# Two additions moved into TensorE's bank, a convolution of fifteen taps, and another order of the opening

## The chip, the core and the metric

The kernel runs on one core of a Trainium2 chip. The core has five engines with queues of their own: TensorE (PE in the profile; its weight loads are PEld), VectorE (DVE), ScalarE (ACT), GpSimd (POOL) and SyncE (SP), which here issues most transfers. Sixteen DMA engines move data between DRAM and the on-chip memory. TensorE writes its results into PSUM, in banks of 512 float32 elements per partition; the other engines read them there.

The metric is the device time of one execution in microseconds (us). The kernel before takes 5532.96 us, the median of three runs (5527.49 to 5539.79 us). The profiled execution took 5528.8 us, and its span from first to last instruction is 5527.0 us.

## The reference

Input x has 4 images of 64 x 64 positions with 96 channels. Layer 0 is a convolution with a selective scan, layer 1 a linear attention with a small network behind it. What matters here, shortened:

```python
# layer 0, on group-normalised x; bilinear(x, W) is sign(x) @ (s * sign(W - mean)).T + b
xz = bilinear(x, W_in, s_in, b_in)           # 96 -> 2 x 192 channels
xp, z = split(xz)
t = sign(xp + move0_b)                       # 192 channels of signs
t = conv3x3(t, sc * sign(conv_W))            # 192 -> 192, padded by one
t = t + conv_b + rp_b0
t = where(t >= 0, t, prelu_a * t)            # PReLU
t = t + rp_b1 + xp                           # residual within the branch
xconv = silu(t)
# four scan directions k over L = 4096 positions: rows, columns, and both reversed
dts, Bs, Cs = bilinear(...)                  # from the signs of xconv
h = exp(dt * A) * h + dt * u * B             # 192 channels x 16 states, per position
y_k = sum over states of h * C, plus D * u
y = sum of the four y_k, layer norm, times silu(z), bilinear back to 96 channels
x1 = x + y
# layer 1
x2 = x1 + attention(layer_norm(x1))          # linear attention: no softmax
out = x2 + ffn(layer_norm(x2))               # fp8-rounded weights and inputs
```

## The kernel before

The program goes through the images ("b", 0 to 3). A prologue for each image makes the scan's inputs (statistics, projection, convolution, sign tables); 1536 scan steps of 128 rows x 1024 positions follow one another without a break; an epilogue for each image does the rest. Prologues and epilogues of other images are generators whose next piece is put between two scan steps. Only the first image's prologue (called alone) and the last image's epilogue have no scan beside them. Every engine works through its instructions in the order in which the program lists them.

The scan step. A tally of each engine's work decides at build time whether the product after a scan goes to VectorE or to GpSimd. Operations called through c.vec and c.gps are counted in it, those called through nc.vector or nc.scalar are not:

```python
lead = c.vec.us - c.gps.us
c.vec.us, c.gps.us = max(0.0, min(lead, 8.0)), max(0.0, min(-lead, 8.0))
pool = c.vec.us + 1.2 > c.gps.us + 2.4
...
c.vec.tensor_tensor_scan(h, dA, w, first, ALU.mult, ALU.add)
if pool:
    self.late = (w, h, cr)                       # GpSimd does w = h * cr in the next step
else:
    c.vec.tensor_tensor(w, h, cr, ALU.mult)
```

On ScalarE the decay dA = exp(dl * anm) of the next step, into one of two PSUM tiles, goes ahead of each scan; GpSimd makes the injection w = dl * bc four steps ahead; TensorE sums the products over the states.

The pools that the change meets (name, buffers):

```python
p = SimpleNamespace(
    w=pool("wp", 9), y=pool("yp", 2), cy=pool("cyp", 2), h=pool("hp", 2), ...
    f=pool("fp", 8), ..., dA=pool("dAp", 2, space=PSUM), ps=pool("psp", 1, space=PSUM),
)
```

The weights, at the start: all loads are issued first, most on SyncE. Those of anm (the scan's A, 24 loads whose runs in DRAM are one element long) are issued on ScalarE's queue:

```python
for g in range(NG):
    src = a["al"][...].rearrange("d k (q j) -> j d (k q)", j=4)
    for j in range(4):
        nc.scalar.dma_start(anm[j::4, g, :], src[j])
```

The prologue's projection. The 192 channels lie as two halves of 96; the signs of each go into a padded image tp of 66 x 66:

```python
for h in range(2):
    for q in range(NQ8):                         # eight pieces of 512 positions
        px, pz = bank(f"ix{h}{q}", 0)[0:96], bank(f"iz{h}{q}", 1)[0:96]
        for ps, c0 in ((px, 96 * h), (pz, DN + 96 * h)):
            nc.tensor.matmul(ps, c.winT[:, c0 : c0 + 96], xsT[:, cols], start=True, stop=True)
        yield
        nc.scalar.activation(tpad[h][...], px..., AF.Sign, scale=..., bias=...)
        sz = f32(f"sz{h}{q}").bitcast(BF16)[0:96, 0:512]
        nc.scalar.activation(sz, pz, AF.Sign, ...)
        c.later.store(c.szd[b][h][:, cols], sz)
```

The convolution, in 16 parts of 96 output channels x 512 positions. A part has 18 matmuls of 96 input channels. The next part's taps are mixed with what is left of the part before:

```python
taps = [(j, t) for j in range(2) for t in range(9)]
...
            nc.tensor.matmul(ps, c.cw[:, j, t, 96 * h : 96 * h + 96], tpad[j][...],
                             start=(j == 0 and t == 0), stop=(j == 1 and t == 8))
...
if s == 0:      # the part before: pz holds sign(x) @ W, v = acs * conv + acb, r = relu(conv)
    c.vec.scalar_tensor_tensor(pz, pz, pv[:, ph, S_X : S_X + 1], v, ALU.mult, ALU.add)
    if alone:
        c.vec.scalar_tensor_tensor(pz, r, c.oma[:, one(ph)], pz, ALU.mult, ALU.add)
elif s == 1 and not alone:
    nc.tensor.matmul(pz, c.omad[:, ph], r, start=False, stop=True, skip_group_check=True)
... # then sign, exp, ln, exp on ScalarE and u = pz * e on VectorE
# after the taps of a part:
v = ...   # VectorE if alone, else ScalarE
r = ...   # ScalarE
pz = ...  # the projection's matmul once more
```

The sign tables. Direction by direction, the signs go to DRAM (sgd), come back as g, are turned by TensorE, and go to DRAM again (gTd), from where the scan loads gT twice, the second time shifted by 16 columns:

```python
nc.sync.dma_start(gw[:, x, 0:48], c.sgd[b][k].rearrange("(p f) -> p f", p=128))
gp = ...                                          # four matmuls with ident8
nc.scalar.activation(t.bitcast(F8), gp[0:48], AF.Copy, saturate=False)
nc.sync.dma_start(c.gTd[b][k], t)
# in the scan:
nc.sync.dma_start(w[0:48], src)
nc.sync.dma_start(w[64:112, :, 0:28], src[:, :, 4:32])
```

The epilogue's last stage, eight pieces of 512 positions for each image:

```python
mm(ps, [(self.ms[2], tt)])                        # the attention's output, plus bias
yield
x2 = f32("x2")[0:96]
c.vec.tensor_tensor(x2, ps, x1, ALU.add)
```

And the opening, in which weights and the first prologue take turns:

```python
made, first = c.weights(), prologue(c, 0, c.xts)
lanes = [made, first]
while (0, 1) not in c.ready:
    interleave(lanes)
    c.later.tick()
```

Of the kernel before, what the change touches and what calls it, by code (L numbers as in the profile page):

```python
# [11 lines left out]
F32 = mybir.dt.float32  # L12
BF16 = mybir.dt.bfloat16
# [40 lines left out]
def hybrid_kernel(ctx: ExitStack, tc: tile.TileContext, a: dict, out: bass.AP):  # L54
# [71 lines left out]
    cw = ctile("cw", [96, 2, 9, DN], F8)  # L126
# [6 lines left out]
    sbias, cbias = ctile("sbias", [96, 2]), ctile("cbias", [96, 2])  # L133
# [24 lines left out]
    def weights():  # L158
# [28 lines left out]
        def transposed(dst, srcs):  # L187

            count[0] += 1
            ps = p.ps.tile([128, 1024], BF16, name=f"tps{count[0]}", tag=f"y{count[0] % 2}")  # L190
            at = 0
            for src in srcs:
                n, f = src.shape
                nc.tensor.transpose(ps[:f, at : at + n], src, identb[:n, :n])
                at += n
            nc.vector.tensor_copy(dst, ps[:f, 0:at], saturate=False if dst.dtype == F8 else None)

# [4 lines left out]
        cwf, cwn = ([[temp(f"{nm}{h}{i}", [96, s.stop - s.start]) for i, s in enumerate(cuts)] for h in range(2)] for nm in ("cwf", "cwn"))  # L202
        for ts, src in ((cwf, a["cw_t"].rearrange("p h t d -> p h (t d)")), (cwn, a["cw_n"])):
            for rows, h, s in halves(src):
                for i, cut in enumerate(cuts):
                    nc.sync.dma_start(ts[h][i][rows], s[:, cut])
# [33 lines left out]
        nc.sync.dma_start(bff[DM : DM + 1, :], a["bff"])  # L240
        nc.scalar.dma_start(pvd, a["pv"][:, :, SD : SD + 3 * NK])
# [6 lines left out]
        for g in range(NG):  # L248
            src = a["al"][32 * (g % 4) : 32 * (g % 4) + 32, g // 4].rearrange("d k (q j) -> j d (k q)", j=4)
            for j in range(4):  # L250
                nc.scalar.dma_start(anm[j::4, g, :], src[j])
# [3 lines left out]
        nc.vector.tensor_tensor(sbias, pv[:, :, B_X], pv[:, :, MOVE0], ALU.add)  # L255
# [4 lines left out]
        transposed(winT, [wis[:, t, :] for t in range(3)])  # L260
        yield
        part = temp("part", [96, 2, 2])
        for h in range(2):
            for i, cut in enumerate(cuts):
                nc.scalar.activation(
                    cw[:, h].rearrange("p t d -> p (t d)")[:, cut], cwf[h][i], AF.Sign, saturate=False
                )
                nc.vector.tensor_reduce(part[:, h, i : i + 1], cwn[h][i], AX.X, ALU.add, apply_absolute_value=True)
# [67 lines left out]
        nc.scalar.activation(anm, anm, AF.Exp)  # L336
        nc.vector.tensor_scalar(anm, anm, -1.0, None, ALU.mult)
# [95 lines left out]
def run(c):  # L433

    made, first = c.weights(), prologue(c, 0, c.xts)
    lanes = [made, first]
    while (0, 1) not in c.ready:
        interleave(lanes)
        c.later.tick()
# [40 lines left out]
def prologue(c, b, xts=None):  # L480
# [11 lines left out]
    with tc.tile_pool(name=f"xg_{b}", bufs=1) as xgp:  # L492
# [3 lines left out]
        with tc.tile_pool(name=f"cv_{b}", bufs=1) as cvp:  # L496
            xsT = cvp.tile([DM, L], F8, name=f"xsT_{b}", tag="xsT")
            tflat = [cvp.tile([96, (IH + 2) * (IW + 2)], F8, name=f"tp{h}_{b}", tag=f"tp{h}") for h in range(2)]
# [58 lines left out]
            for h in range(2):  # L557
                for q in range(NQ8):
                    cols = slice(512 * q, 512 * q + 512)
                    px, pz = bank(f"ix{h}{q}", 0)[0:96], bank(f"iz{h}{q}", 1)[0:96]  # L560
                    for ps, c0 in ((px, 96 * h), (pz, DN + 96 * h)):
                        nc.tensor.matmul(ps, c.winT[:, c0 : c0 + 96], xsT[:, cols], start=True, stop=True)
                    yield
                    nc.scalar.activation(
                        tpad[h][:, 1 + 8 * q : 9 + 8 * q, 1 : 1 + IW], px.rearrange("p (h w) -> p h w", w=IW),
                        AF.Sign, scale=pv[:, h, S_X : S_X + 1], bias=c.sbias[:, h : h + 1], saturate=False,
                    )
                    sz = f32(f"sz{h}{q}").bitcast(BF16)[0:96, 0:512]
                    nc.scalar.activation(
                        sz, pz, AF.Sign, scale=pv[:, h, S_Z : S_Z + 1], bias=pv[:, h, B_Z : B_Z + 1]  # L570
                    )
                    c.later.store(c.szd[b][h][:, cols], sz)
# [4 lines left out]
            taps = [(j, t) for j in range(2) for t in range(9)]  # L577
            one = lambda h: slice(h, h + 1)
            prev = turned = None
            two = c.p.dA.tile([128, CH], F32, name=f"cv2_{b}", tag="dA") if alone else None  # L580
# [24 lines left out]
            for n, part in enumerate(parts + [None]):  # L605
                if part:
                    h, q = part
                    nm = f"{h}{q}"
                    at = 512 * (n % 2)
                    ps = (two[:, at : at + 512] if alone else bank("cv" + nm, 0))[0:96]  # L610
                for s in range(4 if alone else 5):
                    if part:
                        per = 5 if alone else 4
                        for j, t in taps[per * s : min(18, per * s + per)]:
                            dy, dx = divmod(t, 3)
                            nc.tensor.matmul(  # L616
                                ps, c.cw[:, j, t, 96 * h : 96 * h + 96],
                                tpad[j][:, 8 * q + dy : 8 * q + dy + 8, dx : dx + IW],
                                start=(j == 0 and t == 0), stop=(j == 1 and t == 8),
                            )  # L620
                    if s == 0 and turned:
                        by_columns(*turned)
                        turned = None
                    if prev:
                        ph, pq, pz, v, r, pn = prev
                        if s == 0:
                            c.vec.scalar_tensor_tensor(pz, pz, pv[:, ph, S_X : S_X + 1], v, ALU.mult, ALU.add)
                            if alone:
                                c.vec.scalar_tensor_tensor(pz, r, c.oma[:, one(ph)], pz, ALU.mult, ALU.add)
                        elif s == 1 and not alone:  # L630

                            nc.tensor.matmul(pz, c.omad[:, ph], r, start=False, stop=True, skip_group_check=True)
# [37 lines left out]
        with tc.tile_pool(name=f"rw_{b}", bufs=1) as rw:  # L670
# [5 lines left out]
            g2 = rw.tile([128, 2, 320], F8, name=f"g_{b}", tag="g")  # L676
            gw = g2.bitcast(F32)
            for o in (1, 0):
# [74 lines left out]
                if o:  # L753
                    nc.gpsimd.memset(gw[:, :, 48:80], 0.0)
                for x, k in enumerate((o, o + 2)):
                    nc.sync.dma_start(gw[:, x, 0:48], c.sgd[b][k].rearrange("(p f) -> p f", p=128))
                    yield
                    yield
                    gp = bank(f"gp{k}", k // 2).rearrange("p (s f) -> p s f", s=4)
                    for s in range(4):  # L760
                        nc.tensor.matmul(
                            gp[:, s, :], g2[:, x, 48 * s : 48 * s + 128], c.ident8, start=True, stop=True
                        )
                    yield
# [33 lines left out]
class Epilogue:  # L798
# [237 lines left out]
    def last(self, ln):  # L1036
# [22 lines left out]
        while nxt:  # L1059
# [10 lines left out]
            mm(ps, [(self.ms[2], tt)])  # L1070
            yield
            x2 = f32("x2")[0:96]
            c.vec.tensor_tensor(x2, ps, x1, ALU.add)
# [54 lines left out]
class Scans:  # L1128
# [6 lines left out]
    def __init__(self, c):  # L1135
# [10 lines left out]
        self.us, self.gs, self.at, self.loaded, self.sums = {}, {}, -1, set(), {}  # L1146
# [214 lines left out]
    def run(self, back):  # L1361
# [11 lines left out]
        interleave(lanes)  # L1373
        for q in range(NQ):
            self.load_bc(0, self.bt, 0, 0, 0, q)
            self.load_bc(1, self.ct, 0, 0, 0, q)
# [124 lines left out]
```

## Time and profile before

| what | value |
| --- | --- |
| time, median of three | 5532.96 us |
| VectorE busy | 5025.5 us |
| GpSimd busy | 4975.1 us |
| ScalarE busy | 3568.5 us |
| TensorE busy (matmuls) | 3478.7 us |
| first tap of the convolution | 84.1 us |
| first step matmul of the scan's inputs | 233.0 us |
| first scan | 269.6 us |
| last scan step's product ends | about 5410 us |

Busy times are those of the whole profiled execution. A row of the profile's groups names a line of the kernel, an engine, an operation, what it writes and reads ("out<-in"), shapes and count, then the busy time, the mean of one in ns, and the idle time of the engine just before, with what ended it. Line 404 is the tally's helper, so many operations share it and are told apart by their tiles. In a timeline a row has start and duration in us; "SPq" and "ACTq" are transfers being issued, not run.

### The profile page before, as it was taken

How to read it: one execution, taken by the hardware profiler on the slowest of the kernel's cores; microseconds unless marked ns; L12 is line 12 of the kernel's file. 1: busy time of each engine (PE TensorE's matmuls, PEld its weight loads, DVE VectorE, ACT ScalarE, POOL GpSimd, SP SyncE). 2: the span in 40 equal slices, each digit the busy share in tenths (PEclk: the TensorE clock that was granted, in tenths of full speed). 3: DMA queues.
4: the chain of work that ended last, by engine and by line, in shares of the span. 5: the costliest groups of instructions: out<-in, count | busy, mean ns of one | idle time of the engine just before them, and what ended most of it. 6: DMA issues, size and time to landing. Idle time of an engine off the chain costs nothing. (4 is left out here: it accounts for less than half of the span.)

```text
span 5527.0 us, 62184 instructions
## 1 busy us (share of the span) xinstructions
PE 3478.7 (63%) x20133; PEld 1371.3 (25%) x20133; DVE 5025.5 (91%) x3198; ACT 3568.5 (65%) x5568; POOL 4975.1 (90%) x2255
## 2 busy tenths in 40 slices
PE   6456765467645776657665677664677664445677
PEld 2222222122222232222222232221232221111223
DVE  3299999999999999999999999999999999999984
ACT  4467766677666667777666666776556775555554
POOL 2199999899999999999999999999999999999981
PEclk8666776678777776767876777765787565666777
DMA  4455765767666666676765666667666566666652
GB/s 80 120 191 187 211 204 189 237 220 211 200 192 207 197 199 207 195 237 212 223 191 184 206 205 195 198 208 229 201 214 194 179 194 199 213 202 190 204 157 60
DMA packets 613243, 1069.92 MB, mean 194 GB/s; under 512 B 225083, under 2 KB 343924, under 8 KB 611124
## 3 DMA queue, kind: packets, MB, share of 16 engines
q1 hardware_dynamic: 599428, 1065.88, 62.0%
q8 instruction: 158, 2.59, 0.2%
q10 hardware_dynamic: 13488, 0.07, 0.1%
q14 instruction: 169, 1.38, 0.1%
HBM read 833.20 MB, written 229.38 MB: 192 GB/s over the span
## 5 line engine op out<-in xcount | busy, mean ns | idle before, releaser
L404 POOL TENSOR_TENSOR w<-dl,bc 128x1024 f32<-128x1024 f32 x1536 | 3578.8, 2356 | 158.7 <-PE yp L1340 69.6
L1267 ACT ACTIVATE dA<-dl,anm 128x1024 f32<-128x1024 f32 x1536 | 1714.6, 1116 | 495.5 <-DVE w L404 282.7
L404 DVE TENSOR_TENSOR_SCAN dA<-dA,cy,w 128x1024 f32<-128x1024 f32 x711 | 1665.8, 2343 | 98.7 <-ACT dA L1267 94.1
L1340 PE MATMUL yp<-w,sum 128*32 128x256 f32 x12288 | 1289.5, 515 | 401.5 <-POOL w L404 260.0
L404 POOL TENSOR_TENSOR w<-h,bc 128x1024 f32<-128x1024 f32 x587 | 1381.1, 2353 | 114.4 <-DVE h L404 104.2
L404 DVE TENSOR_TENSOR w<-dA,bc 128x1024 f32<-128x1024 f32 x949 | 1162.4, 1225 | 48.7 <-issue 0.9
L404 DVE TENSOR_TENSOR_SCAN h<-dA,cy,w 128x1024 f32<-128x1024 f32 x441 | 1031.6, 2340 | 8.6 <-ACT dA L1267 8.5
L1340 PEld LDWEIGHTS yp<-w,sum 128*32 128x32 f32 x12288 | 316.3, 129 | 1487.4 <-issue 710.4
L1309 ACT COPY cy<-dA 128x1 f32<-128x1 f32 x715 | 112.2, 157 | 747.8 <-DVE w L404 746.2
L404 DVE TENSOR_TENSOR_SCAN dA<-dA,w 128x1024 f32<-128x1024 f32 x238 | 543.3, 2283 | 29.1 <-ACT dA L1267 21.6
L616 PE MATMUL cv<-tp,cw 96*96 96x512 fp8e5 x1152 | 364.4, 452 | 46.2 <-ACT r L656 42.0
L404 DVE TENSOR_TENSOR_SCAN h<-dA,w 128x1024 f32<-128x1024 f32 x146 | 332.5, 2278 | 10.5 <-ACT dA L1267 9.1
L1202 PE MATMUL dps<-gT,wdz 128*128 128x64 fp8e5 x1000 | 113.7, 313 | 339.4 <-ACT ys L1354 310.1
L1215 PE MATMUL dps<-sp,ident 128*128 128x512 f32 x376 | 279.7, 834 | 47.0 <-ACT dps L1211 46.7
L1345 PE MATMUL yp<-ya,back 128*128 128x256 f32 x576 | 239.3, 537 | 1.6 <-DMA ya<-y 1.1
L616 PEld LDWEIGHTS <-cw 96*96 96x96 fp8e5 x1152 | 153.5, 144 | 234.1 <-issue 182.0
L1202 PEld LDWEIGHTS <-wdz 128*128 128x128 fp8e5 x1024 | 95.1, 152 | 427.3 <-issue 395.1
L1202 PE MATMUL dps<-gT,wdy 128*128 128x64 fp8e5 x504 | 59.3, 320 | 204.1 <-ACT ys L1354 202.0
L1309 ACT COPY cy<-h 128x1 f32<-128x1 f32 x437 | 81.4, 186 | 147.5 <-DVE h L404 146.4
L1207 ACT ACTIVATE pd<-dps,dbias,pvd 128x512 f32<-128x512 f32 x188 | 143.2, 761 | 22.6 <-PE dps L1202 22.6
L878 PE MATMUL yc<-eys,mean 96*96 96x512 f32 x240 | 139.2, 734 | 29.2 <-DVE vks L404 13.6
L1345 PEld LDWEIGHTS yp<-ya,back 128*128 128x128 f32 x576 | 123.8, 248 | 130.2 <-issue 93.3
(290 smaller groups left out, 4221.1 us busy)
## 6 DMA issues: line engine op xcount, KB each, us to landing
dl<-dld SPq DMA_DIRECT2D x768, 512.0 KB
bc<-bcd SPq DMA_DIRECT2D x512, 512.0 KB
dld<-pd SPq DMA_DIRECT2D x125, 512.0 KB
yd<-ys SPq DMA_DIRECT2D x768, 64.0 KB
dld<-pd SPq DMA_DIRECT2D x126, 256.0 KB
ya<-yd SPq DMA_DIRECT2D x192, 128.0 KB
pu<-ud SPq DMA_DIRECT2D x32, 512.0 KB
pu<-utd SPq DMA_DIRECT2D x30, 512.0 KB
```

Source lines behind the costliest of these rows:

```text
L404: return getattr(self.eng, name)(out, *args, **kw)
L616: nc.tensor.matmul(ps, c.cw[:, j, t, 96 * h : 96 * h + 96], tpad[j][:, 8 * q + dy : 8 * q + dy + 8, dx : dx + IW], start=(j == 0 and t == ...
L878: self.c.nc.tensor.matmul(ps, w, x, start=(i == 0), stop=(i == len(pairs) - 1))
L1202: nc.tensor.matmul(pv[:, s], wd[:, k, s], gT[:, :, c0 : c0 + 16], start=(s == 0), stop=(s == 7))
L1207: nc.scalar.activation(d[:, 0], ps, AF.Abs, scale=sc, bias=bi)
L1215: nc.tensor.matmul(ps, c.ident, t, start=False, stop=True, skip_group_check=True)
L1267: c.nc.scalar.activation(t, self.dlt[i // NQ][0], AF.Exp, scale=c.anm[:, g, NQ * KORD[e] + q : NQ * KORD[e] + q + 1])
L1309: self.c.nc.scalar.copy(self.carries[g, q], h[:, CH - 1 : CH])
L1340: c.nc.tensor.matmul(y[32 * x : 32 * x + 32, g % 2, :], c.sum4, prod[:, 256 * x : 256 * x + 256], start=(q == 0), stop=(q == NQ - 1 and no ...
L1345: c.nc.tensor.matmul(y[:, g % 2, :], w, src, start=False, stop=(n == len(more) - 1))
```

## The change

It has four parts, which are independent of one another in the code.

1. TensorE adds. In the prologues with a scan beside them, ScalarE multiplies the bank pz by the scale in place, and TensorE adds v (with a unit matrix) and r (as before) into the same bank. In the epilogue's last stage, except for the last image, TensorE adds x1 to the attention's output with a unit matrix, and ScalarE copies the bank out. Neither addition is on VectorE any more.
2. Input channels as 128 and twice 64. The first padded image has 128 channels. The second has the last 64 channels in rows 0 to 63, and once more, shifted by one column, in rows 64 to 127, so that one matmul does two neighbouring taps of a line, and the third tap has zero weights in the upper rows. 9 + 6 = 15 matmuls take the place of 18. The signs of the 64 channels are written twice.
3. The head. Column sums and group means of the first image stand ahead of the work on the weights; the anm loads go to SyncE's queue, and their exp comes later; four of the first image's 16 projections come ahead of the convolution, the others between its taps, in a PSUM tile of their own, with the z signs in the two buffers of the pool h.
4. The first direction's sign table of the first image is copied straight into gT, from two turned copies, instead of through DRAM.

The diff, cut to its core:

```diff
-    cw = ctile("cw", [96, 2, 9, DN], F8)
+    cwA, cwB = ctile("cwA", [128, 9, DN], F8), ctile("cwB", [128, 3, 2, DN], F8)
+    winB = ctile("winB", [DM, 128], F8)
...
-                nc.scalar.dma_start(anm[j::4, g, :], src[j])
+                nc.sync.dma_start(anm[j::4, g, :], src[j])
...
     lanes = [made, first]
+    next(made)
+    for _ in range(6):
+        next(first)
     while (0, 1) not in c.ready:
...
-            tflat = [cvp.tile([96, (IH + 2) * (IW + 2)], F8, ...) for h in range(2)]
+            tflat = [cvp.tile([128, (IH + 2) * (IW + 2)], F8, ...) for h in range(2)]
...
+            two = [c.p.dA.tile([128, CH], F32, name=f"cv{i}_{b}", tag="dA") for i in range(2)] if alone else None
+            def project(h, q):
+                cols = slice(512 * q, 512 * q + 512)
+                if alone:
+                    px, pz = two[1][:, 0:512], two[1][0:96, 512:CH]
+                else:
+                    px, pz = bank(f"ix{h}{q}", 0), bank(f"iz{h}{q}", 1)[0:96]
+                nc.tensor.matmul(px, c.winB if h else c.winT[:, 0:128], xsT[:, cols], start=True, stop=True)
+                nc.tensor.matmul(pz, ...)
+                yield
+                for rows, back in ((slice(0, 64), 0), (slice(64, 128), 1)) if h else ((slice(0, 128), 0),):
+                    nc.scalar.activation(tpad[h][rows, 1 + 8 * q : 9 + 8 * q, 1 - back : 1 - back + IW], ...)
+                sz = c.p.h.tile([128, CH], F32, ..., tag="h") if alone else f32(f"sz{h}{q}")
...
+            if alone:
+                ahead = [project(h, q) for q in range(NQ8) for h in range(2)]
+                for g in ahead[:4]:
+                    next(g)
+                    yield
+                    next(g, None)
+                del ahead[:4]
+            else:
+                for h in range(2):
+                    for q in range(NQ8):
+                        yield from project(h, q)
...
-            taps = [(j, t) for j in range(2) for t in range(9)]
+            taps = [(tpad[0], c.cwA[:, 3 * dy + dx], dy, dx) for dy in range(3) for dx in range(3)]
+            taps += [(tpad[1], c.cwB[:, dy, x], dy, 2 * x) for dy in range(3) for x in range(2)]
...
+                    if alone and ahead:
+                        if s % 2 == 0:
+                            next(ahead[0])
+                        else:
+                            next(ahead.pop(0), None)
...
                         if s == 0:
-                            c.vec.scalar_tensor_tensor(pz, pz, pv[:, ph, S_X : S_X + 1], v, ALU.mult, ALU.add)
                             if alone:
+                                c.vec.scalar_tensor_tensor(pz, pz, pv[:, ph, S_X : S_X + 1], v, ALU.mult, ALU.add)
                                 c.vec.scalar_tensor_tensor(pz, r, c.oma[:, one(ph)], pz, ALU.mult, ALU.add)
+                            else:
+                                nc.scalar.mul(pz, pz, pv[:, ph, S_X : S_X + 1])
                         elif s == 1 and not alone:
-                            nc.tensor.matmul(pz, c.omad[:, ph], r, start=False, stop=True, skip_group_check=True)
+                            for w, x in ((c.i96, v), (c.omad[:, ph], r)):
+                                nc.tensor.matmul(pz, w, x, start=False, stop=True, skip_group_check=True)
...
+                    if alone and k == KORD[0]:
+                        gp2 = columns(1 - k // 2, 0)
+                        nc.scalar.activation(c.gTs[0][0:48], gp[0:48], AF.Copy, saturate=False)
+                        nc.scalar.activation(c.gTs[0][64:112, :, 0:112], gp2[64:112, :, 16:128], AF.Copy, saturate=False)
+                        continue
...
-            mm(ps, [(self.ms[2], tt)])
-            yield
             x2 = f32("x2")[0:96]
-            c.vec.tensor_tensor(x2, ps, x1, ALU.add)
+            if self.alone:
+                mm(ps, [(self.ms[2], tt)])
+                yield
+                c.vec.tensor_tensor(x2, ps, x1, ALU.add)
+            else:
+                mm(ps, [(self.ms[2], tt), (c.i96, x1)])
+                yield
+                nc.scalar.copy(x2, ps)
```

## The prediction

> **What bounds the kernel now.** I read the busy times first, then the stretches, then the groups, and last the timeline of the first 260 us, because the change touches two quite different parts of the program: the long scan, and the opening before it.
>
> ```profile
> PE 3478.7 (63%) x20133; PEld 1371.3 (25%) x20133; DVE 5025.5 (91%) x3198; ACT 3568.5 (65%) x5568; POOL 4975.1 (90%) x2255
> ```
>
> The stretches show where the missing tenth lies. The columns are PE, PEld, DVE, ACT, POOL busy, then clock and DMA.
>
> ```profile
> 240.00:260.00 20.00, 7.74 (x20) 3.58 (x21) 1.89 (x3) 6.61 (x12) 0.64 (x1) 0.59 0.89 300
> ...
> 2250.00:3250.00 1000.00, 644.01 (x3914) 256.05 (x3915) 953.96 (x580) 697.00 (x1083) 957.36 (x419) 0.72 0.66 209
> ```
>
> From about 270 us to 5415 us VectorE (DVE) and GpSimd (POOL) are both 94 to 97% busy. The scan alone must be on VectorE; the product after it goes to whichever of the two has less work by the kernel's own tally. So the pair is the bound, and it is a balanced one. Before 270 us neither does much: that is the opening, a chain of other things. These rows are the pair's work and the two operations that the change takes from it:
>
> ```profile
> L404 POOL TENSOR_TENSOR w<-h,bc 128x1024 f32<-128x1024 f32 x587 | 1381.1, 2353 | 114.4 <-DVE h L404 104.2 <-PE yp L1345 3.0 <-PE yp L1340 1.9
> L404 DVE TENSOR_TENSOR w<-dA,bc 128x1024 f32<-128x1024 f32 x949 | 1162.4, 1225 | 48.7 <-issue 0.9 <-DMA bc<-bcd 0.2
> L404 DVE SCALAR_TENSOR_TENSOR cz<-cz,pv,v 96x512 f32<-96x512 f32 x64 | 47.7, 745 | 1.7
> L404 DVE TENSOR_TENSOR x<-at,x1b 96x512 f32<-96x512 f32 x27 | 18.2, 674 | 4.9 <-PE at L878 4.9
> ```
>
> The opening, by the timeline (start, duration): ScalarE (ACT) issues loads until 30 us and only then computes; the convolution runs from 84 us to 184 us at 5.8 us a part; the sign table gT makes a round trip through DRAM before the first step matmul at 233 us.
>
> ```profile
> 12.15 18.28 ACTq L251 DMA_DIRECT2D anm<-in_al  x24
> 30.48 0.91 ACT L259 ACTIVATE slab<-slab,slab 128x96 bf16<-128x96 f32 x3 [28.46 <-DMA anm<-in_al]
> ...
> 178.01 0.81 DVE L653 TENSOR_SCALAR v<-cv,acs,acb 96x512 f32<-96x512 f32 x1
> 178.85 0.77 ACT L656 ACTIVATE r<-cv,cbias,csc 96x512 f32<-96x512 f32 x1 [1.68 <-DVE v L653]
> ...
> 179.68 4.08 PE L616 MATMUL cv<-tp,cw 96*96 96x512 fp8e5 x18 [1.49 <-ACT r L656]
> ...
> 233.01 1.86 PE L1202 MATMUL dA_s<-gT,wdz 128*128 128x64 fp8e5 x16 [3.10 <-DMA gT<-gTd]
> ```
>
> A convolution part is 18 taps (4.08 us) plus a turn of 1.7 us: v on VectorE, then r on ScalarE, then the next part's taps, which wait for r.
>
> **What the Trainium skill says.** VectorE: DVE Perf Modes, "Why PSUM operands drop a tier": fp32 with an operand in PSUM runs at the plain rate of one element a cycle. The trace fits: 674 to 745 ns for 512 elements a row, so the two adds can't be made cheaper where they are, only moved. PSUM — Partial Sum Buffer, "PSUM bank collisions raise a hardware error": no two engines may touch one bank at once, readers included. The trace fits: r starts 0.03 us after v ends though both only read cv; this turn stays. DMA: Bandwidth & Descriptors, "Issuing engines are not separate DMA queues": all queues end in the same 16 DMA engines, so another issuer saves its own issuing time only. That is what moving the 24 anm loads should do: free 18.28 us of ScalarE and give SyncE the issues. TensorE: Matmul & The Clock Gate, "What's actually happening": the clock is half or whole by recent activity. The trace fits: taps of 0.227 us (4.08/18) in the busy convolution, 452 ns as the mean of all 1152.
>
> **The change part by part. The steady part.** Three later batches have 16 convolution parts each: 48 multiply-adds leave VectorE, 48 x 745 ns = 35.8 us. Three later epilogues have 8 chunks each: 24 adds leave, 24 x 674 ns = 16.2 us. Together 52.0 us (the first batch's 16 and the last batch's keep their form). The tally spreads this: in the two built programs the products on GpSimd go from 587 to 573, those on VectorE from 949 to 963. GpSimd loses 14 x 2353 ns = 32.9 us; VectorE loses 52.0 - 14 x 1225 ns = 34.8 us. The pair thus ends about 33 us earlier if nothing else stands in the way, and with 4 to 5% idle in both nothing much does.
>
> What is added lies on the other two. ScalarE: 48 scalings of a bank at 763 ns (as row v, same shape) 36.6 us; 24 copies at 575 ns (as other PSUM copies of 96x512) 13.8 us; and because the second 64 channels are written twice, shifted by one column, 24 more sign activations at 773 ns, 18.6 us. Sum 69 us on an engine 65% busy. TensorE: 48 x 724 ns for v (rate of the omad matmul) 34.8 us and 24 x 782 ns for x1 18.8 us, less 3 taps x 48 parts x 452 ns = 65.1 us: about 11 us less. TensorE is free anyway.
>
> Where ScalarE is not free is the projection stage. This is its second half in the second batch:
>
> ```profile
> 452.00:480.00 28.00, 18.39 (x96) 4.94 (x88) 24.57 (x14) 24.80 (x39) 27.07 (x12) 0.56 0.49 152
> ```
>
> ScalarE has 24.8 of 28 us already and VectorE is down to 88%. Eight more activations of 773 ns make 31.0 us in 28: this stage must lengthen by 3 us at least and I take 4, thrice: +12 us. Steady part: -33 + 12 = -21 us.
>
> **The opening.** Column sums now stand ahead of the weights on TensorE, ScalarE is free at 12 us instead of 30 us, and only 4 of 16 projections come before the convolution. By engines alone it could start near 52 us. But SyncE now issues every weight load and the 24 anm loads before the first store, and the z signs have two buffers, so the third projection waits for a store. Before, SyncE was through with its loads at 53.9 us; without ScalarE's loads among its own it should be some 6 us quicker, then 24 issues at an estimated 0.4 us (the small wl loads took 0.31 to 0.51 us) make 57 us; eight stores of xb and one of z at 0.5 us, 2 us to land, and the last two sign steps: first tap at about 66 us, not 84.
>
> Then the convolution. Fifteen taps at 0.227 us plus the same turn of 1.7 us make 5.1 us a part, 0.7 us less. But the first six parts carry two projections each, on ScalarE 3.8 us (three tp at 0.77, two z at 0.76) beside the 3.2 us of the part's own five operations; with the waits between them I draw a chain of 8.7 us a part. One part of 6 us, five of 8.7 us, ten of 5.1 us: 101 us, plus 6 us of store waits as now (184 - 84 less 16 x 5.8): 107 us. It ends at 173 us, not 184: -11 us. The direct sign table removes gTd and gT between 226 and 233 us and adds one activation of 0.6 us: -5 us. Everything after it up to the first scan at 270 us is loads that start when it ends, so the shift goes through. Opening: -16 us, and little else.
>
> Sum: -21 - 16 = -37 us, 5533 - 37 = 5496 us.
>
> **The rivals.** First, ScalarE takes the place of the pair: decay (1116 ns, 1536 times) must be one step ahead and stands in ScalarE's order behind the new scalings, which wait for TensorE. For it: VectorE already waits 116 us for decays. Against it: in the convolution stretches ScalarE is 70 to 73% busy with VectorE at 99%, and the scaling stands a step after its matmul. It would give back 20 us or more, time about 5520 us. Second, the opening is bound by loads: the earlier compute only waits for SyncE, whose queue got longer. For it: SyncE's back-to-back issues to 54 us; against it: conv taps wait for no store but by the z buffers. Then the opening gains 5 us, total about 5507 us. Third, the opening gains fully: store waits small, six mixed parts at 7.2 us rather than 8.7, first tap near 55 us: -20 us more, total near 5475 us. Fourth, the projection stage absorbs its extra activations in TensorE's and VectorE's gaps: 12 us better, 5484 us.
>
> **Range and chances.** The steady gain is counted, not guessed (33 us), and the deductions span 0 to 30 us; the opening spans 5 to 36 us. The extremes together give 5464 and 5525; I take 5468 to 5522 for 8 in 10. Two per cent is 111 us, three times what I find, and neither direction has a cause of that size: faster 0.03, same 0.95, slower 0.02.
>
> **What would show it.** Right: VectorE near 4990 us busy and GpSimd near 4942 us, ScalarE near 3637 us; first tap at 60 to 70 us; ten late convolution parts at 5.1 us and the mixed ones above 8; the first step matmul of the scan some 16 us before 233; in the projection stretches of later batches VectorE busy below 88%. Wrong: a first scan no earlier than 265 us (loads bound the opening), VectorE's wait for decays well above 116 us (ScalarE took over), or a span reduced by much more than GpSimd's 33 us plus the opening's shift, which would mean that the moved operations had cost waits that no row of before shows.

## The result, and the profile after

The changed kernel takes 5508.15 us (median of four runs, 5505.96 to 5515.96 us); the kernel before, run beside it, took 5531.23 us. The ratio is 0.9959 with a 95% interval from 0.9941 to 0.9976: 23 us faster, where the prediction had 37 us less. Its 5496 us are 12 us too low; its range, 5468 to 5522 us, holds the measured time. The two profiled executions differ by the same amount (spans of 5527.0 and 5504.2 us), so they can be laid side by side.

The busy times on the page of the kernel after:

```profile
PE 3466.0 (63%) x20089; PEld 1360.3 (25%) x20089; DVE 4996.1 (91%) x3142; ACT 3631.0 (66%) x5673; POOL 4947.3 (90%) x2247
```

VectorE fell by 29.4 us and GpSimd by 27.8 us, ScalarE rose by 62.5 us. The groups of the two kinds of product:

```profile
L421 POOL TENSOR_TENSOR w<-h,bc 128x1024 f32<-128x1024 f32 x573 | 1349.1, 2355 | 124.1 <-DVE h L421 110.0 <-PE yp L1414 5.1 <-DMA dl<-dld 2.3
L421 DVE TENSOR_TENSOR w<-dA,bc 128x1024 f32<-128x1024 f32 x963 | 1179.5, 1225 | 54.7 <-DVE dA L421 0.5 <-DMA bc<-bcd 0.3
```

Fourteen products have changed engine, as the tally said, and the price of one is the same as before (2355 and 1225 ns). The stretches, in the same columns as before (us, then PE, PEld, DVE, ACT and POOL busy, clock, DMA share, GB/s); the first is the second batch's second half of the projection, which now fills 33 us instead of 28:

```profile
454.00:487.00 33.00, 20.11 (x98) 5.17 (x91) 26.86 (x16) 31.82 (x49) 27.96 (x13) 0.54 0.46 152
2250.00:3250.00 1000.00, 637.74 (x3906) 250.45 (x3898) 949.11 (x566) 713.95 (x1111) 953.82 (x417) 0.75 0.65 208
```

To see where 22.8 us of span came from, three points of each trace are enough: the first scan, the end of the last scan step's product, and the end. All times are in us.

| kernel | first tap | first scan | scan stretch | tail | time, median |
| --- | --- | --- | --- | --- | --- |
| before | 84.1 | 269.6 | 5140.0 | 117.4 | 5531.23 |
| after | 71.2 | 271.2 | 5117.7 | 115.4 | 5508.15 |

The scan stretch runs from the first scan to the end of the last product, the tail from there to the end. So the gain is +1.5 (opening) - 22.3 (scan stretch) - 2.0 (tail). The steady part came out near the 21 us predicted; the opening, which was to bring 16 us, brought nothing, though its first tap came 12.9 us earlier. These are the lines of the timeline of after that answer to those of the opening before:

```profile
43.03 18.07 SPq L269 DMA_DIRECT2D anm<-in_al  x24
61.21 4.49 SPq L440 DMA_DIRECT2D xbd<-xb  x8
65.80 21.12 SPq L440 DMA_DIRECT2D szd<-sz  x7
...
231.96 1.91 PE L1271 MATMUL dA_s<-gT,wdz 128*128 128x64 fp8e5 x16
```

The anm loads have left ScalarE (where they took 18.28 us) and take just as long on SyncE, ahead of every store. The first matmul of the scan's inputs starts 1.05 us earlier than before, not 16.

### The profile page after: what moved, and what is told of

Read it like the earlier page. It is cut to its first block, busy times and chain, and to the rows that moved or that the text cites. A ratio compares the mean times of both kernels' runs of the same rounds, so it can differ in the third digit from the quotient of the medians.

```text
span 5504.2 us, 62064 instructions
## 1 busy us (share of the span) xinstructions
PE 3466.0 (63%) x20089; PEld 1360.3 (25%) x20089; DVE 4996.1 (91%) x3142; ACT 3631.0 (66%) x5673; POOL 4947.3 (90%) x2247
## 5 line engine op out<-in xcount | busy, mean ns | idle before, releaser
L421 DVE TENSOR_TENSOR_SCAN dA<-dA,cy,w 128x1024 f32<-128x1024 f32 x726 | 1700.9, 2343 | 90.7 <-ACT dA L1336 75.5
L421 POOL TENSOR_TENSOR w<-h,bc 128x1024 f32<-128x1024 f32 x573 | 1349.1, 2355 | 124.1 <-DVE h L421 110.0
L421 DVE TENSOR_TENSOR w<-dA,bc 128x1024 f32<-128x1024 f32 x963 | 1179.5, 1225 | 54.7 <-DVE dA L421 0.5
L421 DVE TENSOR_TENSOR_SCAN h<-dA,cy,w 128x1024 f32<-128x1024 f32 x426 | 996.7, 2340 | 16.0 <-ACT dA L1336 15.8
L421 DVE TENSOR_TENSOR_SCAN dA<-dA,w 128x1024 f32<-128x1024 f32 x237 | 540.9, 2282 | 36.7 <-ACT dA L1336 28.4
L1284 PE MATMUL dps<-sp,ident 128*128 128x512 f32 x376 | 273.0, 815 | 46.0 <-ACT dps L1280 45.8
L659 PE MATMUL cv<-tp,cwA 128*96 128x512 fp8e5 x576 | 198.4, 470 | 60.3 <-ACT r L706 55.1
L1271 PE MATMUL dps<-gT,wdy 128*128 128x64 fp8e5 x504 | 58.5, 317 | 205.2 <-ACT ys L1423 203.2
L1277 ACT ACTIVATE sp<-dps,dbias,pvd 128x512 f32<-128x512 f32 x188 | 144.2, 767 | 0.0
## 6 DMA issues: line engine op xcount, KB each, us to landing
dld<-pd SPq DMA_DIRECT2D x126, 256.0 KB
ya<-yd SPq DMA_DIRECT2D x192, 128.0 KB
```

Of the source, the lines that this page charges most:

```text
L421: return getattr(self.eng, name)(out, *args, **kw)
L659: nc.tensor.matmul(ps, w[:, 96 * h : 96 * h + 96], tp[:, 8 * q + dy : 8 * q + dy + 8, dx : dx + IW], start=(w is taps[0][1]), stop=(w is t ...
L1271: nc.tensor.matmul(pv[:, s], wd[:, k, s], gT[:, :, c0 : c0 + 16], start=(s == 0), stop=(s == 7))
L1277: nc.scalar.activation(t, ps, AF.Relu, scale=sc, bias=bi)
L1284: nc.tensor.matmul(ps, c.ident, t, start=False, stop=True, skip_group_check=True)
```

## The experiments

My theory after the comparison: the opening is held first by SyncE's 24 loads (they delay the z stores, and with them ScalarE's third z sign), and then, in the convolution, by a ring between VectorE and ScalarE that fewer taps don't shorten. The rival: the loads after the sign table fix the first scan whatever comes before them. For the steady part, the theory: the additions bring what the tally says, and the doubled signs take back 12 us. Its rival: ScalarE's new work costs the scan more than that, or is absorbed.

**The two additions alone, and everything but them.** To the kernel before, only the additions are given; from the changed kernel, only they are taken:

```diff
 # e1, against before; e2 is the reverse of this, against after
-c.vec.scalar_tensor_tensor(pz, pz, pv[...], v, ALU.mult, ALU.add)       # unless alone
+nc.scalar.mul(pz, pz, pv[...])
-nc.tensor.matmul(pz, c.omad[:, ph], r, ...)
+for w, x in ((c.i96, v), (c.omad[:, ph], r)):
+    nc.tensor.matmul(pz, w, x, ...)
-mm(ps, [(self.ms[2], tt)]); c.vec.tensor_tensor(x2, ps, x1, ALU.add)    # unless alone
+mm(ps, [(self.ms[2], tt), (c.i96, x1)]); nc.scalar.copy(x2, ps)
```

> The kernel before with the first part of the change alone: TensorE adds v and x1 in the bank, nothing else. Theory: the balanced pair VectorE and GpSimd sets the time of the scan stretch, so it ends about 33 us earlier (14 products leave GpSimd), with nothing given back, because the projection stage and the opening are as before: about 5500 us, first scan at 269.6 us as before. Rival: the moved operations were hidden or are replaced by waits for ScalarE, and the measured gain came from the convolution with fewer taps or the opening: 5525 us or more.

> The changed kernel with only the first part undone: the two additions are on VectorE again, the fifteen taps, the doubled signs and the new opening stay. Theory: it loses the pair's 33 us and keeps the cost of the doubled sign activations, some 4 us in each of three projection stages: about 5540 us, slower than the kernel before by some 10 us. Rival (the rest of the change carries the gain): 5510 us.

Measured: the additions alone 5514.48 us against 5533.37 of the kernel before, ratio 0.9961 (0.9948 to 0.9973), between the theory's 5500 us and the rival's 5525 us; everything but them 5539.53 us, ratio 1.0012 (1.0006 to 1.0019), as expected. The scan stretch is 5122.9 us in the first and 5145.6 us in the second. The additions are the whole gain, 19 us alone and some 30 us on top of the rest (31 by the times, 29 by the ratios); the rest by itself costs 6 us. In this second kernel the last step's product ends at 5416.4 us instead of 5409.6: 1.3 of these 6.9 us lie ahead of the first scan and 5.6 in the scan stretch; the tail is 1.8 us shorter.

**The 24 loads as one.** The host hands over the same table already in the order of the tile, and one transfer brings it:

```diff
-for g in range(NG):
-    src = a["al"][...].rearrange("d k (q j) -> j d (k q)", j=4)
-    for j in range(4):
-        nc.sync.dma_start(anm[j::4, g, :], src[j])
+nc.sync.dma_start(anm, a["al"])        # [128, NG, 16], only put in order
```

> The changed kernel with the table anm laid out in DRAM as it stands on chip, so that one load takes the place of the 24 loads of single elements that hold SyncE for 18.07 us. Theory: the stall of 12.2 us at the third z sign, where ScalarE waits for a z store behind these loads, disappears; first tap at 57 to 59 us instead of 71.2, and the first scan some 13 us earlier, 258 us: about 5495 us. Rival (the opening is bound by other loads, or by the chain of the convolution, which takes up what is won): first scan still later than 267 us, total 5505 us or more.

Measured: 5498.07 us, ratio 0.9935 (0.9923 to 0.9948), 10 us less than after. First tap at 59.8 us, 11.4 us earlier than after; first scan at 256.0 us, 15.1 us earlier. Its timeline:

```profile
43.84 0.35 SPq L266 DMA_DIRECT2D anm<-in_al  x1
...
57.34 0.76 ACT L597 ACTIVATE sz<-cv,pv 96x512 bf16<-96x512 f32 x1
```

and the same z sign in the kernel after:

```profile
55.73 0.78 ACT L593 ACTIVATE tp<-cv,sbx,pvx 128x512 fp8e5<-128x512 f32 x1 [1.10 <-PE cv L588]
68.71 0.78 ACT L600 ACTIVATE sz<-cv,pv 96x512 bf16<-96x512 f32 x1 [12.20 <-DMA szd<-sz]
```

The bracket says that ScalarE stood still 12.20 us until the first store of a z tile had freed its buffer; that store was behind the 24 loads in SyncE's queue. With one load the sign follows at once. That the shift arrives at the first scan refutes the rival that the later loads have a fixed start: they move with the chain before them.

**v ahead of u in the first convolution.** In the changed kernel VectorE's order is u of part n, then v of part n+1. This puts v first:

```diff
 # first image only
-u = pz * e; store(u); by_columns(u)          # in step 3 of the part before
 nc.vector.tensor_scalar(v, ps, c.acs[...], c.acb[...], ALU.mult, ALU.add)
+u = pz * e; store(u); by_columns(u)          # of the part before
```

> The changed kernel with one pair of VectorE's operations exchanged in the first image's convolution: v of the new part goes ahead of the product u of the part before. Theory: a late part of the first convolution lasts 5.64 us because of a ring of r, second multiply-add, sign, three exponential steps, u, v and again r over ScalarE and VectorE, and not because of its 15 taps; with u out of the ring the parts go to about 5.1 us, ten parts win 5 us, first scan near 266 us. Rival (the taps and the wait for r set the part): parts stay at 5.6 us and the first scan at 271 us.

Measured: 5498.56 us, ratio 0.9936 (0.9923 to 0.9950). The late parts (the ten that carry no projection) take 5.17 us, the first scan is at 263.5 us, 7.6 us earlier than after, where 5 us were expected. This is one late part of the kernel after, with the instructions that hold one another up:

```profile
162.45 0.80 DVE L703 TENSOR_SCALAR v<-cv,acs,acb 96x512 f32<-96x512 f32 x1
...
163.28 0.77 ACT L706 ACTIVATE r<-cv,cbias,csc 96x512 f32<-96x512 f32 x1 [1.47 <-DVE v L703]
...
164.11 2.12 PE L659 MATMUL cv<-tp,cwA 128*96 128x512 fp8e5 x9 [2.00 <-ACT r L706]
...
164.21 0.75 DVE L421 SCALAR_TENSOR_TENSOR cz<-r,oma,cz 96x512 f32<-96x512 f32 x1
165.00 0.59 ACT L641 ACTIVATE sg<-cz 96x512 fp8e5<-96x512 f32 x1 [0.94 <-DVE cz L421]
165.49 0.58 ACT L687 ACTIVATE e<-cz 96x512 f32<-96x512 f32 x1
...
166.77 0.63 ACT L690 ACTIVATE e<-e 96x512 f32<-96x512 f32 x1
...
167.49 0.69 DVE L421 TENSOR_TENSOR u<-cz,e 96x512 f32<-96x512 f32 x1 [2.52 <-ACT e L690]
168.09 0.80 DVE L703 TENSOR_SCALAR v<-cv,acs,acb 96x512 f32<-96x512 f32 x1
```

From one v to the next are 5.64 us. Follow it around: r waits for v; the second multiply-add reads r and starts 0.16 us after its end; the sign waits for that, and exp, ln and exp (the first and the last are shown) follow on ScalarE; u waits 2.52 us for the last of them, and the next v stands behind u. The fifteen taps end at about 167.5 us, when u starts, so v loses only 0.6 us by it; but a faster TensorE would gain nothing more. With v first, the next part's r no longer stands behind this part's exponentials:

```profile
155.20 2.12 PE L659 MATMUL cv<-tp,cwA 128*96 128x512 fp8e5 x9 [1.49 <-ACT r L710]
157.16 1.46 PE L659 MATMUL cv<-tp,cwB 128*96 128x512 fp8e5 x6
160.37 2.12 PE L659 MATMUL cv<-tp,cwA 128*96 128x512 fp8e5 x9 [1.53 <-ACT r L710]
```

The period is 5.17 us, and TensorE's turn is 1.5 us. Ten parts of 5.17 us in place of 5.64 us would be 4.7 us, about the 5 us expected. The rest is another thing. TensorE's granted clock falls to half for 3 us and more at a time in the first convolution, and three of after's late parts last 6.8 us for it. These are the first nine taps of two late parts of after, then the stretches of both (the clock is the column after POOL; 1.00 is the whole clock):

```profile
146.09 3.79 PE L659 MATMUL cv<-tp,cwA 128*96 128x512 fp8e5 x9 [2.00 <-ACT r L706]
...
152.88 2.12 PE L659 MATMUL cv<-tp,cwA 128*96 128x512 fp8e5 x9 [1.49 <-ACT r L706]
...
146.50:149.50 3.00, 3.00 (x9) 1.42 (x8) 0.48 (x2) 2.34 (x4) 0.00 (x0) 0.50 0.82 122
152.88:156.30 3.42, 3.42 (x16) 1.96 (x16) 0.85 (x3) 2.34 (x4) 1.06 (x1) 1.00 0.48 133
```

In this experiment only the first late part has such a stretch (it takes 6.8 us); from 132.5 us to the end of the taps the clock stays whole:

```profile
132.50:179.30 46.80, 33.06 (x147) 17.75 (x145) 25.39 (x36) 27.69 (x45) 9.49 (x9) 1.00 0.40 78
```

What lowers the clock, and whether it stays whole here because of the new order, these traces don't show.

**Nine taps in the first convolution.** A direct test of the ring: the first image's convolution leaves out six of its fifteen taps (those of channels 128 to 191).

```diff
-taps += [(tpad[1], c.cwB[:, dy, x], dy, 2 * x) for dy in range(3) for x in range(2)]
+if not alone:
+    taps += [(tpad[1], c.cwB[:, dy, x], dy, 2 * x) for dy in range(3) for x in range(2)]
```

> The changed kernel with the six taps of the last 64 input channels left out of the first image's convolution only, so that its result for that image is not the reference's and only its time is read. Theory (the ring over ScalarE and VectorE sets the part): the late parts stay at 5.6 us though 1.4 us of taps are gone, and the first scan stays within 3 us of 271 us. Rival (the taps set the part, as the prediction took it): late parts near 4.3 us, first scan near 258 us.

Measured: 5514.11 us in one run; the place of the taps in its timeline says more:

```profile
156.90 3.62 PE L660 MATMUL cv<-tp,cwA 128*96 128x512 fp8e5 x9 [3.25 <-ACT r L707]
162.53 2.12 PE L660 MATMUL cv<-tp,cwA 128*96 128x512 fp8e5 x9 [1.79 <-ACT r L707]
```

A part still begins every 5.63 us, though six taps of 1.46 us are gone. The ring holds it, as the theory has it. The first scan came 4.7 us earlier than after (266.4 us), more than the 3 us that I had allowed: after's three late parts of 6.8 us, each 1.2 us over the ring, are missing. TensorE runs at half clock here too, as the 3.62 us of the first line show, but nine slow taps still fit behind the ring.

**The order of before with one load.** Is the new order of the opening worth anything once the loads are one? The kernel before with the same table and one load on ScalarE's queue:

```diff
-        nc.scalar.dma_start(anm[j::4, g, :], src[j])      # 24 times
+nc.scalar.dma_start(anm, a["al"])
```

> The kernel before with the table anm laid out in DRAM as it stands on chip and loaded at once on ScalarE's queue; its order, its 18 taps and its additions stay. Question: is the new order of the opening worth anything by itself, or were the 24 loads the only obstacle? Theory (the order brings little, because the ring of 5.64 us takes the place of the taps and the mixed parts cost what the projections cost): ScalarE starts some 13 us earlier, the weights' loads come some 10 us earlier, first tap near 73 us, first scan near 258 us, hardly later than the 256.0 us of the changed kernel with one load; about 5521 us. Rival (the order is worth its 16 us): first scan not before 268 us, about 5530 us.

Measured: 5523.12 us, ratio 0.9985 (0.9979 to 0.9992); first scan at 260.2 us, 9.4 us earlier than before. The changed kernel with one load reaches its first scan at 256.0 us, so the new order is worth at most some 4 us there, no more than the first scans of kernels with the same opening differ (below); that it gains anything is not shown. The loads by themselves gain more than twice that, in either kernel.

**The second 64 channels shifted by a transfer.** In the three later batches only one half of the doubled sign activation is left; the shifted copy comes by a transfer inside on-chip memory:

```diff
 # later images only
-for rows, back in ((slice(0, 64), 0), (slice(64, 128), 1)):       # h = 1
+for rows, back in ((slice(0, 64), 0),):
     nc.scalar.activation(tpad[h][rows, ...], AF.Sign, ...)
+nc.sync.dma_start(tflat[1][64:128, 0 : 66 * 66 - 1], tflat[1][0:64, 1 : 66 * 66])
 ...
+yield                          # one step more before the convolution
```

> The changed kernel, in which the shifted copy of the last 64 channels' signs is made by one transfer within the on-chip memory in the three later prologues, in place of 24 sign activations on ScalarE. Theory: the second half of each projection stage is bound by ScalarE (31.8 us busy of 33 us in the changed kernel) and gets its 3.3 to 4 us back, thrice: the scan stretch about 10 us shorter, 5498 us, and VectorE's busy share in these stretches as in the kernel before. Rival (that stage is not bound by ScalarE, or the transfer holds up the convolution behind it): 5505 us or more.

Measured: 5507.70 us, ratio 0.9951 (0.9938 to 0.9963), so no gain over after in the time. In the stage itself it does what it should. In the kernel after, the first and the last sign of the second half and the first taps start here:

```profile
455.03 1.55 ACT L593 ACTIVATE tp<-ix,sbx,pvx 64x512 fp8e5<-64x512 f32 x2
...
482.61 1.55 ACT L593 ACTIVATE tp<-ix,sbx,pvx 64x512 fp8e5<-64x512 f32 x2
...
486.17 1.51 PE L659 MATMUL cv<-tp,cwA 128*96 128x512 fp8e5 x3
```

and in the experiment here:

```profile
452.93 0.76 ACT L594 ACTIVATE tp<-ix,sbx,pvx 64x512 fp8e5<-64x512 f32 x1
...
476.69 0.77 ACT L594 ACTIVATE tp<-ix,sbx,pvx 64x512 fp8e5<-64x512 f32 x1
...
481.11 1.03 PE L663 MATMUL cv<-tp,cwA 128*96 128x512 fp8e5 x3
```

27.58 us against 23.76 us, the figure of before to the hundredth. In the next two batches the stage takes 23.38 and 23.93 us, where after has 25.39 and 27.36 us, so 9.2 us are won in all. They aren't in the total: its scan stretch is 5114.1 us, 3.6 us shorter than after's, and 3.0 us of that are lost in a longer tail (118.3 us). My expectation of 10 us missed. The second half of the rival is visible: from the end of the last sign to the first tap it is 3.65, 2.67 and 1.96 us in the three batches, where after has 2.01, 0.05 and 0.57 us, so 5.7 us of the 9.2 go there. Whether the transfer or the added yield takes them is not shown.

**Additions with fifteen taps in the later convolutions.** The additions brought 19 us alone and some 30 us beside the rest. A theory for this: the saved taps make room on TensorE, so that GpSimd waits less for it. This kernel is e1, and leaves out three of the eighteen taps in the later images' convolution:

```diff
+if not alone:
+    taps = taps[:3] + taps[6:]
```

> The kernel before with TensorE's additions, and in the three later prologues with 15 of 18 taps; three taps are left out there, so the results of those images are not the reference's and only the time is read. Question: why the additions alone won about 20 us and not the 33 us of the count. Theory (TensorE is not idle enough: with 18 taps and the extra passes it frees the scan's buffers later, GpSimd's wait for it rose by 12.6 us): with 15 taps that wait falls back below 72 us and the time to about 5503 us. Rival (TensorE has nothing to do with it; the rest of the count is lost in other waits of the pair): no change against the additions alone, 5512 us or more.

Measured: 5511.51 us, ratio 0.9961 (0.9947 to 0.9975), 3 us from e1. GpSimd's wait for TensorE between 275 and 5380 us:

```profile
POOL w L404 <- PE yp L1350: 82.3, 48, 8.0
```

82.3 us, not below the 79.4 us of e1. The theory falls. Why the additions bring less alone stays open; the intervals of the two gains overlap, so there may be little to explain.

**The three repairs together.** One load, v before u, and the transfer:

> The changed kernel with the one load of anm, v ahead of u, and the shifted copy by a transfer, all three. Theory: they concern a load wait, a ring in the convolution and ScalarE in the later projections, which are different stretches, so their gains add: first scan near 249 us, about 5480 us, one per cent below the kernel before. Rival (with the first two the opening meets another bound, SyncE's stores or the mixed parts): first scan at 255 us or later, about 5488 us.

Measured: 5490.47 us, ratio 0.9919 (0.9905 to 0.9932). This is the fastest kernel of the study, 18 us below the changed one and 42 us below the kernel before. First scan at 247.7 us: 23.5 us before that of after, where the gains of the first two add to 22.7 us. It took 10 us more than the 5480 us expected of it, about what the transfer turned out not to bring. The stages of all runs, in us:

| kernel | first tap | first scan | scan stretch | tail |
| --- | --- | --- | --- | --- |
| e1, additions alone | 85.0 | 273.0 | 5122.9 | 117.7 |
| e2, all but the additions | 71.6 | 270.9 | 5145.6 | 115.6 |
| e3, one load | 59.8 | 256.0 | 5130.3 | 115.7 |
| e4, v before u | 71.0 | 263.5 | 5122.1 | 115.0 |
| e5, shift by transfer | 71.7 | 268.9 | 5114.1 | 118.3 |
| e6, three together | 58.5 | 247.7 | 5120.2 | 115.0 |
| e7, nine taps at first | 71.6 | 266.4 | 5125.9 | 119.9 |
| e8, before with one load | 74.7 | 260.2 | 5143.5 | 117.6 |
| e9, additions, fifteen taps | 84.4 | 273.7 | 5127.1 | 115.6 |

A caution when reading it: after, e3, e4, e6 and e7 have the same scan code with the additions and differ in the opening alone (e6 also in the transfer), yet their scan stretches run from 5117.7 to 5130.3 us. Each is one execution, and a step shifted in time may meet other transfers; why they differ is not shown. Differences of up to 12 us in this column are therefore no evidence. First scans are clearer: before, e1 and e9 have the same opening and lie at 269.6, 273.0 and 273.7 us, after, e2 and e5 at 271.2, 270.9 and 268.9 us. So differences of 4 us say nothing there, those of 7 to 23 us do.

## Why the prediction was partly right

**The pair as the bound: right.** 33 us were counted for the pair's end. GpSimd's products fell by 1381.1 - 1349.1 = 32.0 us (32.9 predicted), VectorE's busy time by 29.4 us (34.8 predicted), and on top of the rest the two additions brought some 30 us.

**ScalarE's new work: right, and a little cheap.** 69 us were predicted, 62.5 us came, because the scaling of a bank took 647 ns, not the 763 ns of a row with two per-partition operands. ScalarE ended at 3631.0 us busy (3637 predicted). TensorE's 11 us less were met (3478.7 to 3466.0 us) by luck: the prediction counted each matmul with its mean duration, though they overlap. Its 1152 taps were 364.4 us busy, which is 316 ns each and not 452, and the additions alone added 42.1 us (e1), not 53.6. The two errors cancel. The 0.227 us that it sets beside the 452 ns are the distance from tap to tap, another measure.

**The first rival, ScalarE as the new bound, didn't happen.** VectorE's waits for the decay between 275 and 5380 us, in the kernel after:

```profile
DVE dA L421 <- ACT dA L1336: 103.9, 73, 7.1
DVE h L421 <- ACT dA L1336: 17.5, 15, 4.4
```

121.4 us in all, where before had 115.8 + 15.8 = 131.6 us.

**The doubled signs: right where they stand, smaller in the sum.** The second half of the projection stage lengthened in the three batches from 23.76, 21.51 and 23.00 us to 27.58, 25.39 and 27.36 us: +3.8, +3.9 and +4.4, together 12.1 us, and 12 were predicted (e1, without doubled signs, has 23.77, 22.18 and 24.43 us, so the last two differences are sure to some 1.4 us). But e2, which has these and not the additions, takes only 6 us more than before (3 to 10.5 by its interval), and taking the signs away again (e5) changed nothing that the time shows. So a part seems to be given back between the stages, which would be the fourth rival in part; how much, and on which engine, the runs don't settle, since scan stretches scatter by as much. Steady part: -21 predicted, -22.3 measured; that they agree so closely is luck, with scan stretches 12 us apart for the same code.

**The opening: wrong, and the second rival came nearer.** The prediction put the first tap at 66 us, the end of the convolution at 173 us, and 16 us less at the first scan. Its terms one by one:

- *"24 issues at an estimated 0.4 us"* was taken from other small loads. They took 0.75 us each (18.07/24), as they had on ScalarE (18.28/24, a line that the prediction shows); moving them moved the cost, and the estimate was 8.5 us short. By luck SyncE's other loads were through at 43.0 us, 4.9 us before the time put for them, so the first tap came at 71.2 us, +5.2. The Trainium skill, DMA: Bandwidth & Descriptors, "Issuing engines are not separate DMA queues", calls the time to initiate a transfer usually small relative to the transfer. How long these transfers run, no trace here shows; but their issue alone held SyncE for 18.07 us.
- *"Ten of 5.1 us"* for the late parts took TensorE's taps plus its turn as the loop. The loop that closes is the ring over VectorE and ScalarE, 5.64 us and independent of the taps (e7), only 0.15 us below the 5.79 us of before, where taps and ring had nearly the same length. Three parts with a stretch at half clock took 6.8 us. Late parts, 128.0 to 187.8 us: 59.8 us, where 51 and 6 for store waits were predicted, +2.8. The "6 us of store waits as now" were misread: in the kernel before, five of the parts take 7.4 to 7.5 us and not 5.8, because their 18 taps take 5.62 to 5.76 us and not 4.08, with the clock at half for a while. The taps of two parts of before:

```profile
128.09:132.17 4.08, 4.08 (x19) 2.33 (x19) 1.44 (x2) 2.34 (x4) 0.00 (x0) 1.00 0.06 16
133.94:139.70 5.76, 5.76 (x19) 2.94 (x19) 1.44 (x2) 2.34 (x4) 1.05 (x1) 0.70 0.03 9
```

  The prediction had named this clock, and took every tap of the convolution at the whole one.
- *"Five of 8.7 us"* and one of 6: the six took 11.2, 9.6, 9.5, 9.1, 8.2 and 9.3 us, 56.8 us where 49.5 were predicted, +7.3. The first is 5.2 us of that. What is left of the work on the weights stands in it, and the copy of woutT, for which VectorE waits, ahead of v:

```profile
80.23 0.29 PE L199 MATMUL tps<-identb,slab 96*96 96x96 bf16 x2 [2.15 <-ACT slab L360]
...
80.55 0.25 DVE L201 COPY woutT<-tps 96x192 bf16<-96x192 bf16 x1 [2.38 <-PE tps L199]
80.73 0.80 DVE L703 TENSOR_SCALAR v<-cv,acs,acb 96x512 f32<-96x512 f32 x1
```

  Of the other five, the one at whole clock took 8.2 us, the four with a stretch at half clock 9.1 to 9.6 us. The chain of 8.7 us was thus near; the weights and the clock were missing.
- *The direct sign table*: right. From the end of the issue of the last store of signs to the scan's first matmul it was 10.4 us and is 5.5 us, -5 as predicted. But the next loads of the scan's inputs (bc) are first issued at 234.41 us, after 233.39 us before, because SyncE still waits for the table of a later direction; the first scan follows 36.7 us after that issue (36.2 before). From this matmul to the first scan it is 2.6 us longer than before.

5.2 + 7.3 + 2.8 + 2.6 = 17.9 us, against the 17.5 us by which the opening missed (-16 predicted, +1.5 measured). The loads and the late parts are one mistake: a duration was put down to the wrong owner, that of the loads to ScalarE's queue, that of a part to TensorE's taps. The prediction's own sign for a wrong opening, a first scan no earlier than 265 us, is what stands in the profile (271.15 us); its words in brackets, "loads bound the opening", are only half right. The issue of loads holds the first tap (e3), the ring, with the half clock, holds the late parts of the convolution (e4, e7), and repairing both moves the first scan by the sum of the two.

**Size.** The 12 us by which 5496 us was too low are, in these two executions, the 17.5 us missing in the opening, less 1.3 us more in the scan stretch, 2.0 us in the tail, and 1.7 us by which the kernel before ran faster beside this one (5531.23 us) than in the runs from which I started (5532.96 us).

## What to carry to other kernels

Before a cost is moved to another queue, ask whether it is the engine's or the transfer's own: these loads of single elements occupied whichever engine issued them, and were cured by the layout in DRAM, not by the issuer. Before a part of a loop is made shorter, follow the brackets once around and add up every ring through the in-order queues; when two rings are nearly equal, shortening one brings only their difference. Before a remainder is called a wait, look at the granted clock in that stretch. And work counted off a balanced pair of busy engines arrived for the most part at the end of the kernel (19 to some 30 us of 33), though a third engine locally got full.

## What the runs showed of the hardware that was not expected

A load of 2 KB as single float32 elements into 32 partitions held its issuing engine for 0.75 us (24 in 18.07 us on SyncE, 18.28 us on ScalarE); the same 48 KB as one load in the tile's order held it for 0.35 us in all. A transfer between on-chip rows took the place of eight activations of 64x512: the stage took 23.76 us, as before the doubling, but the first tap then came 1.4 to 2.6 us later after the last sign, with one step of the generator more between them. In the first convolution, TensorE's granted clock fell to 0.50 for 3 us and more at a time, and nine taps took 3.79 us instead of 2.12; in the late parts of e4 (132.5 to 179.3 us) it did not.
